# Mixture of experts: two half buckets of 768 rows per group become one bucket of 1408 rows with four overflow tiles

## The chip, the cores and the metric

The kernel runs on one core of a Trainium2 chip. The metric is device time in microseconds (us) of one execution; lower is better. Three runs of the kernel before took 3005.65, 3010.7 and 3010.94 us, so its median is 3010.7 us. A profile was taken from a separate execution.

## The reference, cut to what matters

2048 tokens (16 batches of 128 rows, 512 wide) pass through five stages: a state space scan, a cross attention, a ternary feed-forward, a self attention with a gated cross attention, and a mixture of experts, each with a residual and a layernorm. The change is in the last stage:

```python
scores = softmax(x @ gate_w.T); topk_w, topk_idx = top_k(scores, 8)   # 64 experts
w_e = zeros(N, 64).at[arange(N)[:, None], topk_idx].add(topk_w)
flat = w_e[:, inv_map]                      # N x 8 groups x 8 experts
scalar = flat.sum(-1)                       # N x 8: zero where no expert of the group was chosen
soft = softmax(where(flat == 0, -1e9, flat))
xg = x[:, None] + einsum('ngi,ghi->ngh', soft, mask_up_w)
a = silu(einsum('ngh,gih->ngi', xg, gate_proj_w)) * einsum('ngh,gih->ngi', xg, up_proj_w)
y = einsum('ng,ngh->nh', scalar, einsum('ngi,ghi->ngh', a, down_proj_w))
x = layernorm(x + y)
```

A token needs only the groups in which it has an expert, on average two thirds of the eight. Each group has its own weights (gate and up 512 x 352, down 352 x 512, mask_up 8 x 512).

## The kernel before, in words

The 16 batches live in SBUF as `k.x[b]`. `Moe.route` (L1688) takes two batches at a time: it finds the experts, a row's position in each group (`pos`, with the running count `off`), and builds `row`, 776 numbers per token (x, the soft weights split in two for TensorE, and the eight shares). `scatter` (L1792) then writes each batch with one indirect DMA per group from GpSimd (L1797) into `bucket[half][group]`, which holds 768 rows; rows that are not in the group have a destination out of bounds and are dropped. The first eight batches are routed during the attention stage, the other eight in the first units of the expert stage.

`stage_moe` (L1997) works through **units** of two tiles of 128 bucket rows (`pair`): for each half, eight groups of three units (768 rows are 6 tiles). The last group of the second half scatters only batches 8 to 11 (`LAST = 3` tiles: a unit of two and one of one), and works on the `HELD = 4` batches 12 to 15 whole and in place (`placed`, two units). That is 49 units and 97 tiles. One unit is:

- `fetch` (L1821): the rows come in by a DMA from SP, three units ahead;
- `places` and `turn_in` (L1839, L1847): `pts` turns the soft weights, `px` adds the mask product to the turned rows, ScalarE and VectorE copy it to `xgT`;
- `rest` (`pr`, L1874), `gate` (`pg`, L1889; then `pta`, L1899) and `up` (`pu`, L1889): the three matrix products; ScalarE takes silu, VectorE multiplies into `act` (L1905);
- `down` and `store` (`y`, L1913; `yo`, L1926): the product down, scaled by the share, written to `results` by a DMA from ScalarE's queue (L1927).

TensorE's order is pinned: pr(t), pg(t), pta(t), pu(t), pts(t+2), px(t+1), y(t). Half a unit after a tile is stored, `combine` (L1941) has GpSimd gather its results for a batch (`got`, L1935, an indirect DMA; a row that is not in the group reads row 0, which is zero) and add them to `k.x[b]` (L1948). Tile j serves batch j of its half; the last tile of a bucket serves all that remain, so three gathers and adds come at once. After the last group, `combine_last` (L1957) gathers, adds and calls `ended` (L1967), which does a batch's layernorm in pinned VectorE order by `GROUPS` (L1965) and sends it out. The batches of the first half are normalised earlier, by `finish`.

Weights of a group are loaded one group ahead; a mask matrix is prepared by `prepare` (L1660). If a bucket overflows, a flag read on the chip takes a branch at the end (`tc.If(over > 0)`) that does all groups for all batches in place. `clear_rows` (L605) zeroes the buckets in the second stage.

Of the kernel before, what the change touches and what calls it, by code (L numbers as in the profile page):

```python
# [10 lines left out]
F32 = mybir.dt.float32  # L11
# [593 lines left out]
def clear_rows(k, pool):  # L605
# [9 lines left out]
    for h in range(2):  # L615
        for bucket, result in zip(k.bucket[h], k.results[h]):
            k.nc.sync.dma_start(result[0:1], k.zeros[0:1, 0:D])
            for j in range(Moe.TILES):
                k.nc.sync.dma_start(bucket[j * P : (j + 1) * P], k.zeros)
                yield  # L620
# [975 lines left out]
class Moe:  # L1596
# [6 lines left out]
    CAP = 768  # L1603
    TILES = CAP // P
    LAST, HELD = 3, 4

    def __init__(self, k, pp):
# [3 lines left out]
        self.off = [None, None]  # L1611
# [76 lines left out]
    def route(self, p):  # L1688
# [72 lines left out]
        for i in range(2):  # L1761
            off = wr.tile([P, NG], F32, tag=f"r_off{half}", name="r_off", bufs=2)
            if self.off[half] is None:
                nc.vector.tensor_copy(pos[:, i], pc[:, 0, i])
                nc.vector.tensor_copy(off, pc[:, 1, i])
            else:
                nc.vector.tensor_tensor(pos[:, i], pc[:, 0, i], self.off[half], ALU.add)
                nc.vector.tensor_tensor(off, pc[:, 1, i], self.off[half], ALU.add)
            self.off[half] = off
        if p == (NB - self.HELD) // 2 - 1:  # L1770
            self.last = wr.tile([P, 1], F32, name="r_last")
            nc.vector.tensor_scalar(self.last, off[:, NG - 1 :], float(self.CAP - P * self.LAST), None, ALU.add)
        to = wr.tile([P, 2, NG], I32, tag="r_to", name="r_to", bufs=2)
        t = wr.tile([P, 2, NG], F32, tag="r_tt", name="r_tt", bufs=2)
        nc.vector.tensor_scalar(t, ind, -4096.0, 4096.0, ALU.mult, ALU.add)
        nc.vector.tensor_tensor(to, t, pos, ALU.add)
        nc.vector.scalar_tensor_tensor(t, pos, float(self.CAP), ind, ALU.is_lt, ALU.mult)
        nc.vector.scalar_tensor_tensor(self.gidx[:, 2 * p : 2 * p + 2], pos, 1.0, t, ALU.add, ALU.mult)
        if half and p < (NB - self.HELD) // 2:
            at = self.gidx[:, 2 * p : 2 * p + 2, NG - 1 :]  # L1780
            nc.vector.tensor_scalar(at, at, float(P * self.LAST), None, ALU.min)

# [6 lines left out]
        self.sending.append(self.scatter(p, rows, to))  # L1789
        yield  # L1790

    def scatter(self, p, rows, to):  # L1792
        k, nc, half = self.k, self.nc, p // (NB // 4)
        for i, row in enumerate(rows):
            nc.sync.dma_start(k.rows[2 * p + i], row)
            for g in range(self.NG - (p >= (NB - self.HELD) // 2)):
                nc.gpsimd.indirect_dma_start(  # L1797
                    out=k.bucket[half][g][:, :], out_offset=bass.IndirectOffsetOnAxis(ap=to[:, i, g : g + 1], axis=0),
                    in_=row[:, :], in_offset=None, bounds_check=self.CAP - 1, oob_is_err=False,
                )  # L1800
                if g % 2:
                    yield


    def pair(self, h, g, j, n, to=True):
# [434 lines left out]
```

## Time and profile before

| what | value |
| --- | --- |
| median of three runs | 3010.7 us (3005.65 to 3010.94) |
| the profiled execution | 2989.28 us |
| its span, first to last instruction | 2987.5 us |
| TensorE's granted clock over the span | 0.993 |
| last stage: first unit's pr to the end | 2144.6 to 2987.5 us |

The span is what the profile's columns add up in; the profiled execution is 0.7% below the median. TensorE (PE) is busy for most of it. VectorE is DVE, ScalarE is ACT, GpSimd is POOL, SyncE's DMA queue is SP. A matmul of 32-bit floats appears as two instructions in the trace. The chain of waits names, at each moment, the work that the end was waiting for.

### The profile page before, as it was taken

The numbers are of one execution on the slowest core, as the hardware profiler recorded it, in microseconds if no ns is written. First come the engines' busy times: TensorE is split into PE (matmuls) and PEld (weight loads), VectorE is DVE, ScalarE is ACT, GpSimd is POOL, SyncE is SP. The second block draws the span as 40 slices with busy tenths as digits, with TensorE's granted clock in tenths as the row PEclk, the third lists the DMA queues.
The fourth block names the chain that finished last, engine by engine and source line by source line (L and its number), as shares of the span: only waits on it lengthen the run. The fifth ranks groups of instructions, "written<-read, shape, count | busy, mean of one in ns | idle before, by whom it ended". The sixth has DMA issues, their size and how long they took to land.

```text
span 2987.5 us, 41364 instructions
## 1 busy us (share of the span) xinstructions
PE 2892.0 (97%) x14354; PEld 1941.5 (65%) x14378; DVE 1882.1 (63%) x4181; ACT 1322.1 (44%) x3239; POOL 1478.3 (49%) x1264
## 2 busy tenths in 40 slices
PE   8999999999999999999999989999999999999998
PEld 6666665555555555555787556666677777777776
DVE  6999997776676676656887797666652322141213
ACT  6887884333343343345444797555522211111111
POOL 7999996433334334332333664246536653333332
PEclk9999999999999999999999999999999999999999
DMA  7655454870000000014000200224257765464542
GB/s 207 210 136 129 132 134 135 281 261 15 8 11 11 8 11 11 8 54 159 1 1 1 72 1 1 61 102 163 110 201 251 255 220 177 158 206 157 179 152 86
DMA packets 172319, 334.16 MB, mean 112 GB/s; under 512 B 22053, under 2 KB 80933, under 8 KB 170566
## 3 DMA queue, kind: packets, MB, share of 16 engines
q1 hardware_dynamic: 126630, 219.51, 24.0%
q0 software_dynamic: 19840, 66.30, 6.2%
q10 hardware_dynamic: 25632, 45.62, 4.1%
q8 instruction: 116, 1.90, 0.3%
q14 instruction: 101, 0.83, 0.1%
HBM read 245.22 MB, written 139.81 MB: 129 GB/s over the span
## 4 chain that ended last, share of the span: by engine, by line
PE 75%; DVE 14%; ACT 3%; issue 2%; POOL 1%; DMA 1%; SPq 0%; DVEq 0%; ACTq 0%; POOLq 0%
PE y L1913 8%; PE pq L706 7%; PE po L826 6%; PE pu L1889 5%; PE pg L1889 5%; PE pkv L66 4%; PE pr L1874 4%; PE po L1038 4%; PE ao L815 3%; PE sc L775 3%; PE py L66 2%; PE pt L566 2%; PE po L66 2%; PE pg L1018 2%; PE pu L1018 2%
## 5 line engine op out<-in xcount | busy, mean ns | idle before, releaser
L795 POOL TENSOR_TENSOR pr<-pr,sm 128x512 f32<-128x512 f32 x128 | 135.6, 1059 | 367.6 <-DVE sm L794 280.1
L1935 POOL DMA_INDIRECT got<-results,gidx x124 | 119.6, 965 | 392.1 <-DMA results<-yo 366.0
L66 POOL TENSOR_TENSOR dBx<-dtx,BC 128x1024 f32<-128x1024 f32 (+1 forms) x131 | 300.7, 2317 | 17.6 <-DMA BC<-bcd 9.3
L788 ACT ACTIVATE pr<-sc,mx,sf 128x256 f32<-128x256 f32 x256 | 142.4, 561 | 332.7 <-DVE mx L781 304.0
L66 ACT ACTIVATE h<-dt,negA 128x254 f32<-128x254 f32 x512 | 244.1, 477 | 16.7
L826 PE MATMUL po<-w,aT 128*128 128x512 f32 x512 | 233.1, 593 | 0.8 <-DVE aT L820 0.8
L706 PE MATMUL pq<-w,xT 128*128 128x512 f32 x512 | 230.5, 593 | 0.6 <-DVE m L672 0.6
L1913 PE MATMUL y<-dn,act 128*128 128x512 f32 x388 | 182.6, 593 | 3.8 <-DVE act L1905 3.8
L1905 DVE TENSOR_TENSOR act<-pu,act 128x512 f32<-128x512 f32 (+1 forms) x49 | 33.6, 685 | 240.5 <-PE pu L1889 220.7
L66 DVE TENSOR_TENSOR_SCAN h<-h,dBx 128x1024 f32<-128x1024 f32 x72 | 164.9, 2291 | 27.2 <-ACT h L66 22.0
L677 POOL TENSOR_TENSOR m<-m,m 128x512 f32<-128x512 f32 x96 | 122.7, 1278 | 111.9 <-DVE m L672 108.5
L1889 PE MATMUL pu<-xgT,gu 128*128 128x256 f32 (+1 forms) x784 | 177.8, 380 | 0.0
L1889 PE MATMUL pg<-xgT,gu 128*128 128x256 f32 (+1 forms) x784 | 175.5, 377 | 0.0
L1948 POOL TENSOR_TENSOR x<-got,x 128x512 f32<-128x512 f32 x120 | 151.4, 1278 | 46.5 <-DMA got<-results,gidx 45.5
L1926 DVE TENSOR_SCALAR yo<-y,row 128x512 f32<-128x512 f32 x93 | 69.8, 751 | 163.8 <-PE y L1913 160.2
L66 PE MATMUL pkv<-w,cT 128*128 128x512 f32 x368 | 167.3, 597 | 1.3 <-DMA w<-in_x_wvT 1.3
L1028 POOL TENSOR_TENSOR lo<-sg,hi 128x512 fp32r<-128x512 f32 x64 | 84.3, 1319 | 153.4 <-ACT hi L1027 153.3
L826 PEld LDWEIGHTS po<-w,aT 128*128 128x128 f32 x512 | 94.6, 190 | 100.7 <-issue 96.6
L706 PEld LDWEIGHTS pq<-w,xT 128*128 128x128 f32 x512 | 94.0, 190 | 101.3 <-issue 92.3
L1889 PEld LDWEIGHTS pg<-xgT,gu 128*128 128x128 f32 x784 | 146.5, 190 | 17.4
L1889 PEld LDWEIGHTS pu<-xgT,gu 128*128 128x128 f32 x784 | 145.2, 192 | 18.0
L1797 POOL DMA_INDIRECT bucket<-r_row,r_to x124 | 123.0, 992 | 52.7 <-issue 34.9
(408 smaller groups left out, 6886.9 us busy)
## 6 DMA issues: line engine op xcount, KB each, us to landing
bucket<-zeros SPq DMA_DIRECT2D x96, 388.0 KB, 8.0
row<-bucket SPq DMA_DIRECT2D x46, 776.0 KB, 5.7
BC<-bcd SPq DMA_DIRECT2D x128, 256.0 KB, 5.3
results<-yo ACTq DMA_DIRECT2D x93, 256.0 KB, 2.9
gu<-in_moe_guT SPq DMA_DIRECT2D x16, 1408.0 KB, 6.2
x_k<-kv ACTq DMA_DIRECT2D x32, 256.0 KB, 4.7
x_v<-kv ACTq DMA_DIRECT2D x32, 256.0 KB, 5.1
v<-x_v SPq DMA_DIRECT2D x32, 256.0 KB, 2.9
```

Of the source, the lines that this page charges most:

```text
L66: return self.tc.keep_in_program_order(call(*args, **kw))
L677: nc.gpsimd.tensor_tensor(m1, m1, m2, ALU.add)
L706: nc.tensor.matmul(ps, src[:, c], w[c], start=c == 0, stop=c == KC - 1)
L788: nc.scalar.activation(pr[:, j], st.sc[g, i][:, j], AF.Exp, scale=st.sf[:, h : h + 1], bias=st.mx[g, i][:, j : j + 1], accum_out=sm[:, j : ...
L795: nc.gpsimd.tensor_tensor(pr, pr, sm.unsqueeze(2).to_broadcast([P, 2, 2 * P]), ALU.mult)
L826: nc.tensor.matmul(st.po, aT[:, j], k.wo[h // 8][:, h % 8], start=h == 0, stop=h == G * J - 1)
L1018: nc.tensor.matmul(p[:, e], w[:, c, at : at + P], sn.qT[:, :, c], start=c == 0, stop=c == KC - 1)
L1797: nc.gpsimd.indirect_dma_start(out=k.bucket[half][g][:, :], out_offset=bass.IndirectOffsetOnAxis(ap=to[:, i, g : g + 1], axis=0), in_=row[ ...
L1889: self.nc.tensor.matmul(ps[:, e, 0:n], gu[:, c, at : at + P], u.xT[:, c, 0:n], start=c == 0, stop=c == KC - 1)
L1913: self.k.tc.keep_in_program_order(self.nc.tensor.matmul(y, aT, dn[:, c], start=c == 2, stop=c == 1))
L1935: nc.gpsimd.indirect_dma_start(out=got[:, :], out_offset=None, in_=self.k.results[h][g][0:end, :], in_offset=bass.IndirectOffsetOnAxis(ap= ...
L1948: self.nc.gpsimd.tensor_tensor(k.x[b], got, k.x[b], ALU.add)
```

## The change

Both halves now share one bucket of `CAP = 1408` rows (11 tiles) per group, kept as two DRAM tables, for tiles 0 to 4 and 5 to 10. The first pass does tiles 0 to 4 of each group (units of 2, 2 and 1), from the rows of batches 0 to 7; the second pass does tiles 5 to 10 (three units of 2). Rows of batches 5 to 7 whose place is beyond row 640 are scattered a second time into the later table (`remainder`), from the start of the stage.

A row of batch 11 or later whose place is beyond 1408 goes into a table `over`, one tile of 128 rows per group, by a further scatter per batch and group (`EDGE = 11`, groups 0 to 6). `slots` finds on the chip which groups went beyond 1408, up to four, and after each of the groups 3 to 6 of the second pass comes one unit of one tile (`beyond`): its rows and its weights are gathered by indirect DMAs from GpSimd (`pick`, `load_over`) with indices from `slots`, and its results are gathered for batches 11 to 15 (`combine_over`). All four units run whether a group went beyond or not; the branch at the end is taken when they do not suffice. The weights use the buffers of the very first group.

The last group scatters batches 0 to 13 (`LAST = 10`) and does two batches in place (`HELD = 2`), 14 and 15. Batches 0 to 3 are normalised when the first pass ends, 4 to 15 with the last group in new `GROUPS`; batches 9 to 13 are called on in `store`, right after batch 14's result (`found`). Routing of the later eight batches begins one unit earlier.

Tiles per pass: 8 x 5 = 40; then 7 x 6 = 42, 5 of the last group, 4 overflow tiles and 2 in place. That is 93 tiles in 53 units: 40 units of two tiles and 13 of one.

```diff
-    for h in range(2):
-        for bucket, result in zip(k.bucket[h], k.results[h]):
-            k.nc.sync.dma_start(result[0:1], k.zeros[0:1, 0:D])
-            for j in range(Moe.TILES):
-                k.nc.sync.dma_start(bucket[j * P : (j + 1) * P], k.zeros)
-                yield
+    for result in k.results + k.over_results:
+        k.nc.sync.dma_start(result[0:1], k.zeros[0:1, 0:D])
+    for bucket in [b for both in k.bucket for b in both] + [k.over]:
+        for j in range(bucket.shape[0] // P):
+            k.nc.sync.dma_start(bucket[j * P : (j + 1) * P], k.zeros)
+            yield
...
-    CAP = 768
-    TILES = CAP // P
-    LAST, HELD = 3, 4
+    FIRST, TILES, OVER = 5, 11, 4
+    CAP = TILES * P
+    LAST, HELD = 10, 2
+    EDGE = TILES
...
+        if p == NB // 4 - 1:
+            nc.vector.tensor_scalar(off, off, float(self.FIRST * P), None, ALU.max)
...
+        if not half and 2 * p + 1 >= self.FIRST:
+            later = wr.tile([P, 2, NG], I32, tag="r_la", name="r_la", bufs=2)
+            nc.vector.tensor_scalar(pos, t, float(self.FIRST * P), 8192.0, ALU.is_lt, ALU.mult)
+            nc.vector.tensor_tensor(t, t, pos, ALU.add)
+            nc.vector.tensor_scalar(later, t, float(-self.FIRST * P), None, ALU.add)
+            self.later += [(rows[i], later, i) for i in range(2) if 2 * p + i >= self.FIRST]
+        over = None
+        if 2 * p + 1 >= self.EDGE:
+            far = self.far[:, 2 * p - self.EDGE + 1 : 2 * p - self.EDGE + 3]
+            nc.vector.tensor_scalar(far, pos, float(1 - self.CAP), 0.0, ALU.add, ALU.max)
+            nc.vector.tensor_tensor(far, far, ind, ALU.mult)
+            over = self.fixed.tile([P, 2, NG], I32, tag="r_ov", name="r_ov", bufs=2)
+            nc.vector.tensor_scalar(pos, t, float(self.CAP), 8192.0, ALU.is_lt, ALU.mult)
+            nc.vector.tensor_tensor(t, t, pos, ALU.add)
+            nc.vector.tensor_tensor(over, t, self.const[:, 2].unsqueeze(1).to_broadcast([P, 2, NG]), ALU.add)
...
+    def scatter(self, p, rows, to, over):
+        k, nc = self.k, self.nc
         for i, row in enumerate(rows):
-            nc.sync.dma_start(k.rows[2 * p + i], row)
-            for g in range(self.NG - (p >= (NB - self.HELD) // 2)):
-                nc.gpsimd.indirect_dma_start(
-                    out=k.bucket[half][g][:, :], out_offset=bass.IndirectOffsetOnAxis(ap=to[:, i, g : g + 1], axis=0),
-                    in_=row[:, :], in_offset=None, bounds_check=self.CAP - 1, oob_is_err=False,
-                )
+            b = 2 * p + i
+            nc.sync.dma_start(k.rows[b], row)
+            for g in range(self.NG - (b >= NB - self.HELD)):
+                self.put(k.bucket[g][b // (NB // 2)], row, to, i, g)
+                if b >= self.EDGE and g < self.NG - 1:
+                    self.put(k.over, row, over, i, g)
...
+    def remainder(self, row, to, i):
+        for g in range(self.NG):
+            self.put(self.k.bucket[g][1], row, to, i, g)
+            if g % 2:
+                yield
...
+    def slots(self):
+
+        nc, pool, NG, S = self.nc, self.fixed, self.NG, self.OVER
+        off = self.off
+        ex = pool.tile([P, NG], F32, name="ov_ex")
+        nc.vector.tensor_scalar(ex, off, float(self.CAP), None, ALU.is_gt)
+        nc.vector.memset(ex[:, NG - 1 :], 0.0)
+        rank = ex
+        for step in (1, 2, 4):
+            more = pool.tile([P, NG], F32, name=f"ov_rank{step}")
+            nc.vector.tensor_copy(more, rank)
+            nc.vector.tensor_tensor(more[:, step:], rank[:, step:], rank[:, : NG - step], ALU.add)
+            rank = more
...
+        for s in range(S):
+            nc.vector.scalar_tensor_tensor(self.one[:, s], rank, float(s + 1), ex, ALU.is_equal, ALU.mult)
+            nc.vector.tensor_scalar(least[:, s], rank, float(s), None, ALU.is_le)
...
+        for s in range(S):
+            own = pool.tile([P, n, NG], F32, tag="ov_own", name="ov_own")
+            nc.vector.tensor_tensor(own, self.far, self.one[:, s].unsqueeze(1).to_broadcast([P, n, NG]), ALU.mult)
+            row = pool.tile([P, n], F32, tag="ov_row", name="ov_row")
+            nc.vector.tensor_reduce(row, own, AX.X, ALU.add)
+            nc.vector.tensor_scalar(self.back[:, s], row, float(P), None, ALU.min)
...
+    def pick(self, out, table, s, i, rows=P):
+
+        self.nc.gpsimd.indirect_dma_start(
+            out=out, out_offset=None, in_=table, in_offset=bass.IndirectOffsetOnAxis(ap=self.at[0:rows, s, i : i + 1], axis=0)
+        )
+
+    def load_over(self, s):
+
+        nc, a, I, wr = self.nc, self.k.args, self.I, self.wr
+        gu = wr.tile([P, KC, 2 * I], F32, tag="gu", name="gu")
+        dn = wr.tile([P, 3, D], F32, tag="dn", name="dn")
+        raw = self.wk.tile([P, D], F32, tag="got", name="mup_raw", bufs=8)
+        self.over_w[s] = gu, dn
+        flat = lambda t: t.rearrange("g r c -> (g r) c")
+        for c in range(KC):
+            self.pick(gu[:, c], flat(a["moe_guT"]), s, c)
+        self.pick(raw[:, :], flat(a["moe_mup"]), s, 7)
+        yield
+        mup = self.over_mup[s] = wr.tile([P, D], F32R, tag="raw", name="mup_over")
+        for c in range(3):
+            rows = P if c < 2 else I - 2 * P
+            self.pick(dn[0:rows, c], flat(a["moe_downT"]), s, KC + c, rows)
+        nc.sync.dma_start(dn[I - 2 * P :, 2], self.k.zeros[0 : 3 * P - I, 0:D])
+        yield
+        nc.scalar.copy(mup, raw)
+        nc.vector.tensor_tensor(raw, raw, mup, ALU.subtract)
+        yield
+        nc.vector.tensor_scalar(raw, raw, self.part[:, 1:2], None, ALU.mult)
+        nc.vector.scalar_tensor_tensor(mup, mup, self.part[:, 0:1], raw, ALU.mult, ALU.add)
...
+    def beyond(self, s):
+
+        u = Ctx()
+        u.s, u.n, u.to = s, 1, [self.k.over_results[s][1:, :]]
+        return u
+
     def fetch(self, u):
         u.row = self.wk.tile([P, 2, self.ROW], F32, tag="row", name="row", bufs=self.depth)
+        if u.s is not None:
+            self.pick(u.row[:, 0], self.k.over[:, :], u.s, 7)
+            return
...
+            own = self.wk.tile([P, self.NG + 1], F32, tag="own", name="own", bufs=1)
+            self.nc.vector.tensor_tensor(own[:, 1:], u.row[:, 0, D + 4 * self.E :], self.one[:, u.s], ALU.mult)
+            self.nc.vector.tensor_reduce(own[:, 0:1], own[:, 1:], AX.X, ALU.add)
+            shares = [own[:, 0:1]]
...
-                self.ended(u.b + i)
+                for b in (*self.found, u.b + i):
+                    self.ended(b)
+                self.found = []
...
+    def combine(self, g, b):
+
+        got = self.result(g, b)
+        for _ in range(3):
+            yield
+        self.add(b, got)
+        if g == self.NG - 1 and b < self.FIRST - 1 and b % 2:
+            for _ in range(6):
                 yield
-            self.finish(b - 1, k.tc.keep_in_program_order)
-
-    def combine_last(self, ns):
-
-        k = self.k
-        found = [self.gather(1, self.NG - 1, n) for n in ns]
-        for b, got in found:
-            self.nc.gpsimd.tensor_tensor(k.x[b], got, k.x[b], ALU.add)
-        for b, _ in found:
-            self.ended(b)
-
-    GROUPS = (8, 9), (10, 11, 12), (13, 14, 15)
+            self.finish(b - 1, self.k.tc.keep_in_program_order)
+
+    def combine_over(self, s, b):
+        got = self.gather(self.k.over_results[s][:, :], self.back[:, s, b - self.EDGE + 1 : b - self.EDGE + 2])
+        for _ in range(3):
+            yield
+        self.add(b, got)
+
+    def combine_last(self, bs):
+
+        for b, got in [(b, self.result(self.NG - 1, b)) for b in bs]:
+            self.add(b, got)
+
+    GROUPS = (4, 5, 6), (7, 8), (9, 10), (11, 12, 13), (14, 15)
...
+        for q in range(2 * NG):
+            h, g = divmod(q, NG)
+            first[len(units)] = q
+            lo, hi = (m.FIRST, m.LAST if g == NG - 1 else m.TILES) if h else (0, m.FIRST)
+            for j, n in cuts(lo, hi):
+                units.append(m.pair(g, j, n))
+                units[-1].q = q
+            s = q - 2 * NG + 1 + m.OVER
+            if 0 <= s < m.OVER:
+                units.append(m.beyond(s))
+        m.sending += [m.remainder(*job) for job in m.later]
         units += [m.placed(NG - 1, b, 2) for b in range(NB - m.HELD, NB, 2)]
-        units[0] = m.opened
-        per = T // 2
+        units[-1].q = 2 * NG - 1
...
+            if u.s is not None:
+                for b in range(m.EDGE, NB):
+                    running.append(m.combine_over(u.s, b))
+                return
             j = u.j + i
-            if u.h and u.g == NG - 1:
-                m.combine_last(range(j, j + 1 if j < m.LAST - 1 else H - m.HELD))
-            else:
-                for n in range(j, j + 1 if j < T - 1 else H):
-                    running.append(m.combine(u.h, u.g, n))
+            if u.g == NG - 1 and j >= m.FIRST:
+                bs = list(range(j, j + 1 if j < m.LAST - 1 else NB - m.HELD))
+                m.combine_last(bs)
+                m.found += bs
+                if j < m.LAST - 1:
+                    for b in m.found:
+                        m.ended(b)
+                    m.found = []
+                return
+            for b in range(j, j + 1 if j < T - 1 else NB):
+                running.append(m.combine(u.g, b))
+            if u.g == NG - 1 and j == m.FIRST - 1:
+                m.found += [j]
...
+            if t + 3 == start[NG]:
+                assert not (m.now or m.sending or k.to_route)
+                running.append(m.slots())
+            if t == start[NG] + 5:
+                over = nc.values_load(m.flag, min_val=0, max_val=1)
+                running.append(m.load_over(0))
+            if unit(t - 1) and units[t - 1].s is not None and units[t - 1].s + 1 < m.OVER:
+                running.append(m.load_over(units[t - 1].s + 1))
...
+                u.w = weights[u.q] if u.s is None else m.over_w[u.s]
...
-    k.bucket = [[dram.tile([Moe.CAP, Moe.ROW], F32, name=f"bucket{h}{g}") for g in range(Moe.NG)] for h in range(2)]
-    k.results = [[dram.tile([Moe.CAP + 1, D], F32, name=f"results{h}{g}") for g in range(Moe.NG)] for h in range(2)]
+    cut = Moe.FIRST * P
+    k.bucket = [[dram.tile([n, Moe.ROW], F32, name=f"bucket{g}{i}") for i, n in enumerate((cut, Moe.CAP - cut))] for g in range(Moe.NG)]
+    k.over = dram.tile([Moe.NG * P, Moe.ROW], F32, name="over")
+    k.results = [dram.tile([Moe.CAP + 1, D], F32, name=f"results{g}") for g in range(Moe.NG)]
+    k.over_results = [dram.tile([P + 1, D], F32, name=f"over_results{s}") for s in range(Moe.OVER)]
```

## The prediction

> **What bounds the kernel now.** I read the page first: TensorE is busy for 97% of the span, and three quarters of the chain of waits is TensorE.
>
> ```profile
> PE 2892.0 (97%) x14354; PEld 1941.5 (65%) x14378; DVE 1882.1 (63%) x4181; ACT 1322.1 (44%) x3239; POOL 1478.3 (49%) x1264
> PE 75%; DVE 14%; ACT 3%; issue 2%; POOL 1%; DMA 1%; SPq 0%; DVEq 0%; ACTq 0%; POOLq 0%
> ```
>
> A share of the span says little about one stage, so next came the busy time by window in the expert stage. The columns are PE, PEld, DVE, ACT, POOL, clock, DMA share, GB/s.
>
> ```profile
> 2460.00:2600.00 140.00, 140.00 (x654) 108.72 (x653) 26.79 (x42) 18.69 (x44) 51.74 (x47) 1.00 0.52 176
> 2660.00:2940.00 280.00, 279.29 (x1302) 214.69 (x1301) 63.35 (x117) 36.72 (x87) 102.76 (x93) 1.00 0.49 165
> ```
>
> TensorE idles 0.71 us in 420; VectorE and GpSimd are idle for three quarters and two thirds. The stage is as long as its matmuls, so a tile costs what its matmuls cost. The chain near the end holds both kinds of unit, two tiles (from 2919.49) and one tile (from 2935.45):
>
> ```profile
> 2919.49 2.60 PE pr L1874 x16
> 2922.09 3.45 PE pg L1889 x16
> 2925.54 0.22 PE pta L1899 x2
> 2925.76 3.46 PE pu L1889 x16
> 2929.22 0.22 PE pts L1843 x2
> 2929.44 0.40 PE px L1854 x4
> 2929.83 0.46 PE px L1860 x4
> 2930.29 5.15 PE y L1913 x12
> 2935.45 1.30 PE pr L1874 x8
> 2936.75 1.78 PE pg L1889 x16
> 2938.53 0.11 PE pta L1899
> 2938.64 1.79 PE pu L1889 x16
> 2940.43 0.22 PE pts L1843 x2
> 2940.64 0.47 PE px L1854 x4
> 2941.12 0.87 PE px L1860 x8
> 2941.99 2.58 PE y L1913 x6
> ```
>
> pts and px work for later units, so the third pair of rows is that of the one-tile unit (0.40 + 0.46) and the last that of two tiles (0.47 + 0.87). Two tiles: 2.60 + 3.45 + 0.22 + 3.46 + 0.22 + 0.47 + 0.87 + 5.15 = 16.44 us; the y rows of the quiet second half lie 16.45 apart, and I use that. One tile: 1.30 + 1.78 + 0.11 + 1.79 + 0.11 + 0.40 + 0.46 + 2.58 = 8.53, that is 0.30 over half of two.
>
> **The change, part by part.** *Tiles.* Before: 48 x 16.45 + 8.53. After: 40 x 16.45 + 13 x 8.53. Difference 8 x 16.45 - 12 x 8.53 = 131.6 - 102.4 = 29.2 us less. An overflow unit turns soft weights twice: 4 x 0.11 = 0.4 back. **-28.8.**
>
> The pg row speaks for the one-tile unit: 16 instructions in 1.78 us against 3.45, 111 ns each against 216. [...]
>
> *The end.* Before, only two batches are normalised after the last unit's first y. After, batch 14's product releases, in pinned VectorE order, the norms of 9 to 13, 14 and 15. The last unit's pr begins at 2960.80; batch 14's sum follows 12.60 us later (2973.40). From the end of the chain: a sum takes 0.78 with its gap, statistics 0.95 a batch (2976.76 to 2977.71), a group's inverse root 2.36 (2977.71 to 2980.07). So 12.60 + 0.78 + 7 x 0.95 + 3 x 2.36 + 0.78 = 27.9 against 19.25 (2980.05) before: +8.6. One ScalarE pass fewer follows (0.72): **+7.9.** GpSimd doesn't set this: the gather came 3.1 us after the one-tile unit's y (2947.68 - 2944.57); five at 1.27 and five adds at 1.24 end at 3.1 + 6.3 + 6.2 = 15.6, before batch 13's turn near 19.6.
>
> *Norms of 4 to 8.* They fall in the last group's units. The root of (4, 5, 6) stands on VectorE ahead of `rest` of the one-tile unit: 0.75 + 0.95 + 2.36 + 0.36 = 4.4 us after its start, where pta is due at 1.30 + 1.78 = 3.1: 1.4 us. Adds still queued on GpSimd can hold it longer, up to 11 x 1.24 = 13.6. I take **+3** (0 to +15), nearer the queue's empty end, because GpSimd idles two thirds now.
>
> *Collisions.* One row shows VectorE held by GpSimd:
>
> ```profile
> 2221.01 5.37 DVE L1749 TENSOR_TENSOR r_ex<-r_ex,r_on 128x128 f32<-128x128 f32 x1
> 2221.27 4.95 POOL L1948 TENSOR_TENSOR x<-got,x 128x512 f32<-128x512 f32 x4
> ```
>
> The same instruction takes 0.28 to 0.29 otherwise; here it ends with GpSimd's four adds, `act` is late, and TensorE idles 3.1 us. The first pass now ends a group with one gather, not three: **-3.1** (0 if another burst takes its place). In the second pass the bursts grow to six adds (7.4 us) and five, and VectorE gets two-input work there: two in `load_over` and `own`, 12 in all. At 3.1 each that is 37 us, with the 6.5 us that VectorE idles ahead of `act` in a two-tile unit it is nothing. I take **+3**, a quarter of a hit per overflow unit's three, nearer the idle row.
>
> *Small things.* `route` gets some 3 to 10 tiny VectorE instructions per pair (0.17 to 0.44 us each) and `slots` about 40; they lie in VectorE's idle time ahead of `act`, which is only 3 us in a one-tile unit: **+1.5** (0 to +8, one microsecond for each such unit of the first pass). The 24 second scatters open the stage on GpSimd: **+1.5** (0 to +25, see the rivals). Twelve result rows are zeroed at once, 5 us of SP's queue at 516 us; TensorE waits there for no load: 0 (to +5). Data volume hardly grows: the software queue's 66.30 MB less 124 gathers of 0.26 MB is 33.8 MB, about 10900 rows of 3.1 KB, the rows that the routing picks; so out-of-range rows move nothing.
>
> *GpSimd's own load.* First pass: 24 + 62 + 35 scatters at 1.28 (0.98 and 0.30 of issue) and 40 gathers with adds at 2.51 make 255 us; the pass is 16 x 16.45 + 8 x 8.53 + some 18 of routing = 350. Covered. Second pass, group with overflow unit: 16 gathers and adds 40.2, nine picks at 1.28 (a scatter's row) 11.5, together 51.7 of 3 x 16.45 + 8.53 = 57.9. Covered, by little; GpSimd is busy 37% of this time now. The first pick is queued three units ahead of its use, the weights four.
>
> *Sum.* -28.8 + 7.9 + 3 - 3.1 + 3 + 1.5 + 1.5 = **-15.0 us** on the profiled 2989.3. I carry the difference to the median: 3010.7 - 15.0 = **2995.7**.
>
> **Rivals.** *Full cover:* VectorE and GpSimd hide everything but the tail: 3010.7 - 28.8 - 3.1 + 7.9 = 2986.7. For it: VectorE is busy only 20 to 23% of the second pass (the windows above). Against: the `r_ex` row.
>
> *Stalls eat it:* hits on every overflow unit (12 more), the norms held by bursts (6 more): -15 + 18 gives 3014; half of it 3005. For it: two-input work meets larger bursts. Against: most of it lands where VectorE idles.
>
> *GpSimd becomes the bound (slower):* place, the second pass from group 3; the price is a pick of 128 rows of 2816 bytes. From (57.9 - 40.2) / 9 = 1.97 us a pick, GpSimd no longer ends its work in the period, the overflow rows and weights come late and TensorE waits. At 3 us it falls behind by 4 x 9 x 1.03 = 37: 3010.7 - 15 + 37 = 3033. For it: 90% of GpSimd's time is spoken for, in order, with waits for results between. Against: a scatter of 3104 bytes a row takes 0.99, a gather of 2048 bytes 0.97, so the row's length hardly counts.
>
> *The opening:* the 24 scatters come ahead of GpSimd's last attention add (2158.07) and its two clears, for which the first rows and `rest` wait: 24 x 1.28 = 31 less the 6.2 us that it idles there: 3010.7 - 15 + 25 = 3021. From 17 scatters ahead the gain is gone. Against: the adds stand first in the program.
>
> *The change doesn't do what it says:* the four tiles don't suffice and the branch redoes everything: 64 units x 16.45 = 1053 more, 4049. Counted from the reference's inputs (drawn with seed 0), three groups exceed 1408 rows (1461, 1415, 1469, below 1536), and the last group has 1236 of 1280 rows before its held batches: very unlikely.
>
> **How the numbers follow.** Forecast 0.62 (2989 to 3003); full cover 0.08; stalls 0.14 (2999 to 3014); GpSimd 0.10; opening 0.05; branch 0.01. Faster by over 0.2% (below 3004.7; about what a measurement of this kernel can tell) is 0.62 + 0.08 + 0.05 of the stalls = 0.75; same is the other 0.09; slower 0.16. The range leaves out the slower cases and the lowest ends: 2982 to 3011.
>
> **What would show it.** Right: y rows of one-tile units 8.5 us apart, 93 tiles; the stage's TensorE time down by 29; no `r_ex` above 1.5 us; after the last y, a chain of VectorE norms near 12.7 us (27.9 - 15.2) instead of 4.1. Wrong: TensorE waiting for `row`, `gu` or `pts` at an overflow unit (GpSimd late); picks far above 1 us; y waiting for `act` in the second pass; a longer gap at the stage's start; or pg of one tile far above 1.78, which would undo the tile price.

## The result, and the profile after

The changed kernel took **3052.7 us** (median of four executions, 3044.5 to 3054.5), the kernel before 3009.0 beside it: ratio 1.0141, 95% interval 1.0119 to 1.0163. It is 43.8 us slower, where 15 us faster was predicted. The profiled execution took 3051.1 us. First the lines of its page that answer to those of before:

```profile
PE 2892.9 (95%) x14422; PEld 1942.0 (64%) x14446; DVE 1896.3 (62%) x4280; ACT 1327.2 (44%) x3267; POOL 1618.2 (53%) x1405
PE 60%; DVE 13%; DMA 3%; ACT 3%; issue 3%; POOL 3%; another core or an unknown queue 1%; SPq 0%; DVEq 0%; POOLq 0%; ACTq 0%
```

TensorE's share of the chain of waits fell from 75% to 60%; what came in is DMA, GpSimd, and two names that stand for "nothing the profile shows": "issue" and "an unknown queue". To place the loss I divided each profile at five events: GpSimd's first and last add of the gated attention, the first unit's last y, the last y of the first pass, the last y of all. Of the rows below only the first three belong here; the others are experiments. Times in us.

| profile | to first add | gated attention | to first y | first pass | second pass | end | span |
| --- | --- | --- | --- | --- | --- | --- | --- |
| before | 1892.0 | 267.3 | 17.0 | 396.9 | 402.7 | 11.6 | 2987.5 |
| before_again | 1897.7 | 270.8 | 17.1 | 407.7 | 402.9 | 11.6 | 3007.9 |
| **after** | 1896.8 | 288.7 | 18.1 | 351.1 | 475.3 | 19.3 | 3049.3 |
| late_remainder | 1898.2 | 270.6 | 19.6 | 367.1 | 475.8 | 19.4 | 3050.7 |
| mup_late | 1896.1 | 282.5 | 17.8 | 349.8 | 465.5 | 19.2 | 3030.9 |
| both | 1898.5 | 269.6 | 23.9 | 352.6 | 465.7 | 19.4 | 3029.6 |
| no_remainder | 1896.5 | 270.0 | 18.1 | 342.5 | 477.0 | 19.4 | 3023.5 |
| sp_weights | 1900.9 | 285.5 | 18.0 | 351.3 | 475.0 | 19.3 | 3050.0 |
| fill_puts | 1896.3 | 291.7 | 18.1 | 334.0 | 475.9 | 19.2 | 3035.3 |
| fill_all | 1896.6 | 290.6 | 16.4 | 339.5 | 476.0 | 20.8 | 3039.9 |
| first_spread | 1896.8 | 267.7 | 18.1 | 338.8 | 474.2 | 19.4 | 3014.9 |
| second_spread | 1901.7 | 280.1 | 17.0 | 338.1 | 438.7 | 18.9 | 2994.5 |
| both_spread | 1895.6 | 269.8 | 16.6 | 335.1 | 438.6 | 18.8 | 2974.7 |

Against before_again, a second profile of the kernel before at its usual time: gated attention +17.9, first pass -56.6 (the prediction's terms give about -65), second pass +72.4 (the tiles alone: +34.6), end +7.7.

*Gated attention.* GpSimd's timeline; the number in brackets is idle time ahead of the instruction:

```profile
2148.53 0.97 POOL L1824 DMA_INDIRECT bucket<-r_row,r_la  x1 [0.30 <-issue]
2149.80 0.97 POOL L1824 DMA_INDIRECT bucket<-r_row,r_la  x1 [0.30 <-DVE gate L1515]
2151.08 0.98 POOL L1824 DMA_INDIRECT bucket<-r_row,r_la  x1 [0.30 <-issue]
2152.07 1.07 POOL L1490 TENSOR_TENSOR at_s<-at_s,sm 128x512 f32<-128x512 f32 x1
...
2156.87 0.97 POOL L1824 DMA_INDIRECT bucket<-r_row,r_la  x1 [0.31 <-issue]
2157.86 1.29 POOL L1516 TENSOR_TENSOR x<-x,gate 128x512 f32<-128x512 f32 x1
```

The second scatters (`r_la`), which the program calls for at the start of the expert stage, stand between the attention's `at_s` and `x`: GpSimd works on `at_s` and `x` with no idle time ahead of them, so they were due earlier. The `gate` that the last line's `x` reads is done at 2149.65; the add starts 8.2 us later, behind five scatters and two `at_s`.

*Second pass.* After each of the first three overflow units a unit takes 24.4, 24.1 and 25.9 us instead of 16.4, and one of 23.2 stands ahead of the first. The timeline of the first of them:

```profile
2765.44 0.94 POOL L2069 DMA_INDIRECT got<-results,gidx  x1 [1.75 <-DMA results<-yo]
...
2777.93 0.95 POOL L1886 DMA_INDIRECT mup_raw<-in_moe_mup,ov_at  x1 [0.30 <-issue]
...
2781.67 0.62 ACT L1908 CAST mup_over<-mup_raw 128x512 fp32r<-128x512 f32 x1 [11.33 <-DMA mup_raw<-in_moe_mup,ov_at]
2782.20 0.59 ACT L2023 ACTIVATE act<-pg 128x512 f32<-128x512 f32 x1
...
2782.68 0.36 ACT L2028 COPY aT<-pta 128x256 f32<-128x256 f32 x1
...
2783.10 0.79 PE L1981 MATMUL px<-soft,mup 128*128 128x256 f32 x2 [5.54 <-ACT aT L2028]
```

Read it from below: TensorE waits 5.54 us for `aT`; `aT` stands on ScalarE behind `mup_over`; that copy has waited 11.33 us for the pick of `mup_raw`; and the pick was issued at 2777.93 as the last of a row of GpSimd's, six gathers from 2765.44 on and four picks of `gu`. The copy's wait began at 2770.34, 7.6 us before the pick was issued, and the first matmul that reads `mup_over` starts at 2817.97, 36 us after the copy. Over the second pass, by the list of waits (us in all, times, longest):

```profile
PE px L1981 <- ACT aT L2028: 17.5, 3, 6.1
ACT mup_over L1908 <- DMA mup_raw<-in_moe_mup,ov_at: 41.5, 4, 11.9
```

### The profile page after: what moved, and what is told of

It reads as the page before. It is cut to its first block, busy times and chain, and to the rows that moved or that the text cites. A ratio compares the mean times of both kernels' runs of the same rounds, so it can differ in the third digit from the quotient of the medians.

```text
span 3049.3 us, 41951 instructions
## 1 busy us (share of the span) xinstructions
PE 2892.9 (95%) x14422; PEld 1942.0 (64%) x14446; DVE 1896.3 (62%) x4280; ACT 1327.2 (44%) x3267; POOL 1618.2 (53%) x1405
## 4 chain that ended last, share of the span: by engine, by line
PE 60%; DVE 13%; DMA 3%; ACT 3%; issue 3%; POOL 3%; another core or an unknown queue 1%; SPq 0%; DVEq 0%; POOLq 0%; ACTq 0%
PE y L2048 7%; PE pq L706 7%; PE po L826 6%; PE pu L2016 4%; PE po L1038 4%; PE pg L2016 4%; PE pr L2001 3%; PE ao L815 3%; PE sc L775 3%; PE pt L566 2%; PE pg L1018 2%; PE pu L1018 2%; PE pT L803 1%; PE ps L1427 1%; PE pk L706 1%
## 5 line engine op out<-in xcount | busy, mean ns | idle before, releaser
L2080 POOL TENSOR_TENSOR x<-got,x 128x512 f32<-128x512 f32 x146 | 183.5, 1273 | 66.4 <-DMA got<-results,gidx 64.1
L2048 PE MATMUL y<-dn,act 128*128 128x512 f32 x372 | 179.6, 606 | 12.3 <-DVE act L2032 12.3
```

Of the source, the lines that this page charges most:

```text
L2048: self.k.tc.keep_in_program_order(self.nc.tensor.matmul(y, aT, dn[:, c], start=c == 2, stop=c == 1))
L2080: self.nc.gpsimd.tensor_tensor(self.k.x[b], got, self.k.x[b], ALU.add)
```

## The experiments

They were made in five sets; in each, before ran beside them on the same chip. In the first three sets (three chips) before took 3005.6 to 3009.9 us, in the last two (two other chips) 2988.0 and 2990.3. So a time is told with its ratio to before of its own set. The record doesn't name the chip of after and of the first profile of before.

**Set 1 (before 3009.9 us).** Four kernels. The first is before, unchanged.

> The kernel before, unchanged, profiled once more. In the trace of the changed kernel, TensorE's semaphore events come up to 7.5 us after the end of the matmul that sets them, 111 of them over 0.5 us late, all after 1986 us; in the trace of before none is. The profiled execution of before is also 20 us under its median (2989.3 against 3009.0), that of after is not (3051.1 against 3052.7). Theory A (the late wake-ups are something that executions of both kernels have, and the one profiled execution of before happened to lack): this profile has some, its span lies near 3005, and 15 to 20 us of the 62 between the two profiles are no effect of the change. Theory B (the change brings them): again none, and a span near 2988.

3009.7 us, span 3007.9, 49 late wake-ups by the count that gives 111 in after: theory A. (Some 30 records of TensorE's steps are missing in this profile and some 50 in after, so part of either count is steps without a record.) The profile that the prediction was made from lacked some 20 us that the timed executions have. The table shows where: 3.5 us in the gated attention, 10.8 in the first pass, nothing in the second. Another 5.7 lie ahead of the first add; there the profiles of the last two sets, which have no late wake-ups, differ as much (1892.7 to 1901.7), so hold-ups account for some 14 of the 20.

`late_remainder`:

```diff
-        m.sending += [m.remainder(*job) for job in m.later]
+        m.sending.append(m.remainders())     # each put inside issue_after(the clearing of rest)
```

> The changed kernel with one edit: the 24 second scatters are held behind the clearing of the expert stage's spare tiles, so that none stands in GpSimd's order ahead of the attention stage's last adds. Theory A (they stood in the way of those adds): the last add of the attention stage comes at about 2163 us and not at 2184, nearly all of that reaches the end, and the time is 3030 to 3036 against 3052.7; GpSimd then has 31 us of scatters at the start of the expert stage, which may give back up to 5. Theory B (the stage is longer because of late wake-ups, whatever GpSimd's order): the add comes at 2175 or later and the time falls by less than 8.

3047.5 us, ratio 1.0109 (1.0082 to 1.0137). The attention stage is mended as theory A says (270.6), but the time is not: the first pass is 16.0 longer. In the new place the 24 scatters run for 31 us in one piece (from 2169.5), and this is what TensorE and ScalarE do near its end:

```profile
2192.14 0.27 PE L1703 MATMUL pl<-gw,r_x 128*128 128x64 f32 x1 [1.88 <-issue]
...
2194.24 0.26 PE L1703 MATMUL pl<-gw,r_x 128*128 128x64 f32 x1 [1.83 <-issue]
...
2194.96 0.58 ACT L1994 COPY xgT<-px 128x512 f32<-128x512 f32 x1 [10.25 <-remote]
```

TensorE waits for nothing that the profile shows and yet issues one matmul in 2 us; ScalarE idles 10.25 us for a release ("remote") that no instruction's end accounts for. This made theory C, below.

`mup_late`:

```diff
+        self.pick(raw[:, :], flat(a["moe_mup"]), s, 7)      # now ahead of the four picks of gu
...
+        yield
+        yield
+        keep(nc.scalar.copy(mup, raw))
```

> The changed kernel with one edit: of the picks of an overflow tile's weights the one for mup goes first, and ScalarE's and VectorE's work on it stands later in their order, just over a unit ahead of the tile's own turn. Theory A (the second pass loses 31 us because ScalarE's copy of mup waits for a pick that stands behind six gathers and four picks on GpSimd, and ScalarE's later work waits behind the copy): the losses of 6.8, 8.0, 7.6 and 9.5 us at the four places go, 24 to 31 us in all, and the time is 3022 to 3030. Theory B (it is GpSimd's load itself, with its gathers, picks and adds in bursts, and the wait would only show at another place): less than 8 us are won.

3028.5 us, ratio 1.0054 (1.0037 to 1.0071): 24 us under after, inside theory A's range, but not for its reason. Only the first of the four places is whole in its profile, and the second pass is 9.8 us shorter; of the 18.4 us between the two spans 6.2 lie in the gated attention, which the edit doesn't touch. The units after the three overflow units take 24.6, 25.6 and 21.0 us, little less than in after, now with this:

```profile
2835.15 0.60 ACT L2024 ACTIVATE act<-pg 128x512 f32<-128x512 f32 x1 [10.28 <-remote]
```

`both` joins the two edits:

> The two edits together. If both theories A hold, the gains add: 42 to 52 us, 3001 to 3011, the time of the kernel before, give or take 0.3%. If one alone holds, 3022 to 3036. If the late wake-ups decide, over 3036.

3031.0 us, ratio 1.0066 (1.0049 to 1.0083). The gains don't add; the same waits without a visible releaser are there (VectorE's `act`: 47.4 us in four pieces for "remote", 12.3 in three in after), and the first unit's last y ends 23.9 us after the attention's last add, in after 18.1.

**Set 2 (before 3005.6).** Theory C measured by itself, in the kernel before:

```diff
+                self.nc.gpsimd.indirect_dma_start(     # table: 8 spare ones in turn; every index is 8192
+                    out=table[:, :], out_offset=bass.IndirectOffsetOnAxis(ap=self.outside[:, 0:1], axis=0),
+                    in_=self.k.ident[:, :], in_offset=None, bounds_check=P - 1, oob_is_err=False,
+                )
...
+            if t == 36:
+                m.nowhere(24)                  # burst
+            if 30 <= t < 42:
+                m.nowhere(1)                   # spread, in both halves of a unit
```

> The kernel before with one addition in a quiet place: in the second pass (unit 36 of 49) GpSimd issues 24 indirect scatters in one run, of 128 rows each, all of whose places lie outside the table, so that no row moves; nothing waits for them and the output is unchanged. Theory C (a long unbroken run of GpSimd's indirect transfers itself holds up the wake-ups and the issue of the other engines, whatever it moves): TensorE, ScalarE and VectorE stand for some 8 to 17 us inside the 31 us of the run, with waits that no instruction ends, and the time rises by 8 to 17 us over before (3009.9), to 3018 to 3027. Theory D (the stalls come of the bytes on the DMA rings, of the buffers or of GpSimd's in-order queue): gathers and adds come up to 31 us late, which 9 buffers cover, and the time rises by less than 3.

> The same 24 empty scatters in the kernel before, one in each half of units 30 to 41, between the gathers and adds that stand there. Theory C: there is no long run, and the time stays within 3 us of before (3007 to 3013). A theory C' (each indirect transfer costs the others its 0.5 us, however it is spaced) expects the same rise as the run in one piece, 8 to 17. Theory D: within 3 us.

`burst` took 3030.4 us, ratio 1.0082 (1.0065 to 1.0099): **24.8 us for 24 transfers that move nothing.** `spread` took 3006.1, ratio 1.0003 (0.9994 to 1.0013). Theory C, with more than its 8 to 17 us, and not C'. (That rows out of range move nothing is the prediction's estimate: before's scatters moved some 10900 rows of the 124 x 128 = 15872 that they name. Here every place is out of range.) TensorE's, ScalarE's and SP's timelines of burst, whose run goes from 2795.90 to 2826.61:

```profile
2809.39 2.76 PE L1874 MATMUL pr<-gu,xgT 128*128 128x192 f32 x16
2811.06 7.44 ACTq L1927 DMA_DIRECT2D results<-yo  x2
2834.16 0.33 ACT L1878 ACTIVATE rest<-pr 128x192 f32<-128x192 f32 x1 [28.92 <-remote]
```

```profile
2794.59 23.89 SPq L1825 DMA_DIRECT2D row<-bucket  x2
```

A line with x2 goes from the start of the first issue to the end of the second. One issue of `results` by itself takes 0.33 us (at 2793.92), in before one of `row` 0.38 (median; 1.18 at most), so what is late is the second. `rest` starts 22.0 us after the end of the products that it reads (2812.15), and 7.6 us after the run's end. The unit takes 37.4 us instead of 16.4.

> The changed kernel without the 24 second scatters; left out are the rows of blocks 5 to 7 whose place in a group is 640 or more, so the output is not the full one. With the scatters held behind the attention stage (the run late_remainder) the attention stage was 18.1 us shorter and the first units 16.0 longer. Theory C: the same 24 transfers cost 16 to 18 us in either place, and without them the time is 3052.7 - 17 = 3033 to 3037. Rival: what was lost in the first pass there had another cause (a late gather, a late weight), and the time here is that of late_remainder, 3042 to 3050.

3022.5 us, ratio 1.0056 (1.0039 to 1.0073): 30 us less than after, or 26.8 by the two distances to before (43.8 and 17.0). In the profiles 18.7 of it is in the gated attention and 8.6 in the first pass. That is more than the 16 to 18 us that theory C expected; the 8.6 us in the first pass are put down to the run, which is argued.

`sp_weights` loads the overflow weights by SyncE:

```diff
-            self.pick(gu[:, c], flat(a["moe_guT"]), s, c)
+        nc.sync.dma_start(gu, a["moe_guT"][s].rearrange("(c p) i -> p c i", p=P))
+        nc.sync.dma_start(raw, a["moe_mup"][s])
```

> The changed kernel with the weights of the four overflow tiles loaded by SyncE from groups 0 to 3 and not picked by GpSimd from the groups found (32 picks less, four rows' picks remain); the bytes are the same, only rows of overflow tiles are computed with other weights than they should be. Theory C (eight picks more in one run with six gathers make it long enough to hold up the other engines; taking mup's copy out of the way removed the wait for the pick at the first tile only): the losses of 6.8, 8.0, 7.6 and 9.5 us at the four places go, 26 to 32 us, and the time is 3021 to 3027. Theory D (the bytes of the weights beside those of the gathers): the losses stay, less than 8 us are won.

3043.0 us, ratio 1.0121 (1.0105 to 1.0138); the second pass stays at 475.0, as theory D's number has it. But ScalarE's copy, left in its place, still waits 31.1 us in three pieces (the profile puts one down to `mup_raw`, two to `over_results<-yo`). At the first overflow unit SyncE issues `mup_raw` at 2758.40 and the copy starts at 2769.25. So who issues the transfer changes little as long as the copy stands close behind (31.1 us of waits for 41.5 in after); against bytes as the reason speaks `second_spread` below, on another chip, which makes as many transfers as after and whose second pass takes 438.7 us, 1.4 over before's 402.7 and the tiles' 34.6.

**Set 3 (before 3006.5).** Pauses instead of moves: a clearing of 512 bytes on one partition (0.51 us) behind each indirect transfer.

```diff
+        with tc.issue_after(dma.ins):
+            self.pause = nc.gpsimd.memset(self.pad, 0).ins      # the next transfer is queued behind it
```

> The run burst (24 empty scatters in one piece in the kernel before, which cost 24.8 us against before), with a short clearing of 512 bytes on one partition by GpSimd behind each of them, some 0.3 to 0.6 us by the clearing of 256 words in 0.28 us at the stage's start. Theory C as a rate (indirect transfers asked for at 1.28 us each, without a pause, are more than what serves them can take, the excess piles up and others wait; a little slower they are taken): the rise falls to 0 to 6 us, 3006 to 3012. Theory C as a count (24 without other long work between is too many, at this pace or a little slower): 15 to 25 us remain, 3020 or more.

3007.7 us, ratio 1.0005 (0.9992 to 1.0018), and no unit beside the run takes over 16.5 us in its profile. With half a microsecond of other work behind each of the 24 there is next to nothing left of the 24.8 us of set 2: a rate, not a count, if burst would have cost as much on this chip. It wasn't run here; for it speaks that before takes 3006.5, as in set 2.

> The changed kernel with the same short clearing behind each scatter, scatters kept in the order of the program, and the 24 second ones row by row, so that they come to stand partly between the first units' gathers. Theory C (rate): the attention stage and the first pass lose what they lose to runs of scatters, 18 us and some 10 us, as in the run without the second scatters (3022.5): 3010 to 3024. Rival (GpSimd's own time is what counts there: 88 clearings in the attention stage and the opening lengthen its work by some 40 us, and its adds end that stage): 3035 or more.

3038.8 us, ratio 1.0118 (1.0097 to 1.0139): in the rival's range. The first pass is the shortest of all (334.0), as theory C has it, but the gated attention is longer (291.7 us; 288.7 in after). The rival puts this down to GpSimd's own time: its 88 clearings, at the 0.51 us that one takes, are an estimated 45 us more in the attention stage and the opening.

> The run mup_late (3028.5) with the clearing behind every indirect transfer, scatter, gather and pick. Theory C (rate): the second pass also keeps some 25 us, and the time is 2985 to 3002, under the kernel before. Rival (the second pass's losses behind the overflow tiles are of the bytes or of ScalarE's order): no more than the scatters' share, 3004 to 3012. Rival (GpSimd's longer queue): 3012 or more.

3043.6 us, ratio 1.0134 (1.0113 to 1.0155): worse than mup_late's 1.0054. GpSimd is busy 356 of the second pass's 476 us (264 of 475 in after), and VectorE's `own` waits 39.0 us in four pieces for the rows of the overflow tiles. The last rival, GpSimd's longer queue, is right here.

> The kernel before with the clearing behind each scatter and gather. Its one quiet profile is 20 us under its usual time, and its usual profile (the run before_again) has 58 late wake-ups, all beside runs of scatters. Theory C (rate): 2985 to 2997. Rival (these late wake-ups are chance, or the longer queue costs what the pauses give): 3000 to 3012.

2996.1 us, ratio **0.9970 (0.9958 to 0.9981)**: the pauses alone make the kernel before faster by 10.5 us. In its profile the first pass takes 395.5 us (407.7 in before_again), the gated attention 277.2 (270.8).

**Set 4 (before 2990.3).** Spreading without pauses where GpSimd is loaded. In `second_spread`:

```diff
+        picks((raw[:, :], flat(a["moe_mup"]), s, 7))       # then a yield
+        picks(*gus[:2])                                    # and so on: five halves of units
...
+                    running.append(m.combine_over(u.s, b, (b - m.EDGE) // 2))
+                running.append(m.combine(u.g, b, (b - j) // 2))
```

> The changed kernel with the 24 second scatters behind the attention stage, row by row between the first units' gathers, and with the clearing behind each of them and behind each scatter of the expert stage; the scatters of the attention stage are as they were. Theory C (runs hold the others up; the attention stage lost 18 us to the 24 that stood in it, the first pass some 17 to its runs): the attention stage takes 270 us, the first pass 334 to 340, and the time is 3052.7 - 18 - 14 = 3018 to 3024. Rival (the 24 cost their 16 us wherever they stand, as in late_remainder, paced or not): 3034 or more.

> The changed kernel with the second pass's transfers of an overflow tile spread: its eight picks go out over five halves of units and not two, mup's copy stands a unit later, and the gathers of the last tile of a group and of an overflow tile go out in twos, a half apart, behind the adds before them. The number of transfers is the same. Theory C (the 23 to 25 us that stay at the four places are runs of up to 20 transfers): the second pass goes from 475 to 445 us or less, and the time is 3018 to 3028. Rival (GpSimd has too much to do there at any order: 25 transfers of 1.28 us and 16 adds of 1.27 us in the 58 us of such a group, 52 us): the losses stay or move, and the time is over 3030, no better than mup_late's 3028.

> Both edits together. If theory C is the cause in both stretches, the gains add, 3052.7 - 32 - 28 = 2985 to 2998, under the kernel before (3006.5). If one alone holds, 3016 to 3028.

> The run burst with 12 empty scatters in one piece and not 24. In burst the last wake-up that came in time was at 2810 us, 16 us and 12 transfers into the run. If a run costs only what comes after that point, 12 cost 0 to 4 us. If each transfer of a run costs the same, 12 cost half of 24.8 us, 10 to 14.

`first_spread` 3017.4 us, ratio 1.0098 (1.0074 to 1.0121); `second_spread` 2989.2, 0.9995 (0.9981 to 1.0010); `both_spread` **2978.1, ratio 0.9962 (0.9949 to 0.9975)**, 12.2 us under before and the fastest of all; `burst12` 2991.2, 1.0005 (0.9995 to 1.0016). In these four profiles there are 0 to 1 late wake-ups, and burst12 is no test of length, since before has none either. But the second pass of first_spread is as long as ever (474.2), and its waits in the second pass name the copy:

```profile
PE px L1996 <- ACT aT L2043: 17.0, 3, 6.2
```

```profile
ACT mup_over L1923 <- DMA mup_raw<-in_moe_mup,ov_at: 34.4, 3, 12.0
```

(the numbers: us in all, times, longest). In second_spread TensorE's longest wait there is another:

```profile
PE y L2058 <- DVE act L2042: 1.1, 1, 1.1
```

So on this chip the second pass's loss is the order of two queues and not the hold-up by runs. Which of the edits does it, the later copy, the spread picks or the spread gathers, isn't separated: mup_late ran on a chip with hold-ups only.

**Set 5 (before 2988.0).**

> The run burst once more (24 empty scatters in one piece in the kernel before), beside burst12. If the kernel before takes about 3006 us here: 3026 to 3036, as at first. If it takes about 2990: theory C as a property of any chip expects 10 to 25 us over it; theory E (the hold-up shows on some chips or in some placements only, those on which the kernel before takes 3006) expects less than 3.

> The run burst12 once more (12 in one piece), beside burst. If the kernel before takes about 3006 us here: 0 to 4 us over it if only what comes after some 12 transfers of a run counts, 10 to 14 if each transfer of a run costs the same. If it takes about 2990: less than 3, as at first.

`burst_same` 2991.1 us, ratio 1.0012 (1.0000 to 1.0024), `burst12_same` 2989.3, 1.0000 (0.9990 to 1.0010). That is nearer theory E: the run that cost 24.8 us on one chip costs 3.2 by the medians on another, just over the 3 that E allowed and far from C's 10. In the profile of burst_same no unit beside the run takes over 16.5 us.

## Why the prediction was wrong, point by point

- **Tiles, -28.8: right.** In after a one-tile unit takes 9.1 us behind a two-tile unit of 16.0, 25.1 together, and 16.45 + 8.53 = 24.98 was said. In both_spread, where little else is left, the passes are 61.8 shorter and 35.9 longer than in the quiet profile of before.
- **The end, +7.9: right.** 11.6 became 19.3, +7.7.
- **Norms of 4 to 8, +3: low.** The last group's second and third unit take 21.9 and 10.2 us for 16.4 and 8.5: +7, held by GpSimd's adds (a norm's statistics wait up to 9.4 us for one), inside the range given. In both_spread it is +1.
- **Collision gone, -3.1: right.** `r_ex` takes 1.15 us at most. (VectorE's share in the two windows of the prediction is 19 and 23%, not 20 to 23.)
- **The second scatters "open the stage on GpSimd": +1.5: wrong.** The rival had the mechanism and nearly the price (25; 26.8 without the scatters, of which it didn't foresee the part in the first pass), and was given 0.05, "against: the adds stand first in the program". The failing step is this sentence: the order on GpSimd was not that of the program. Moving them out of the attention stage shortens that stage by 10.3 us without hold-ups (280.1 to 269.8), by 18.1 with them (288.7 to 270.6).
- **"Covered, by little ... The first pick is queued three units ahead of its use, the weights four": wrong, and the largest error.** The picks are as cheap as said (0.95 us against a bound of 1.97), GpSimd has the time (busy 264 of the second pass's 475 us), and in that pass TensorE's two waits are for `aT` and `act`, none for `row` or `gu`. (In the code the weights of the later three tiles are queued three units ahead, not four.) But the use that counted wasn't the tile's matmul; it was the first instruction that reads the pick, ScalarE's copy, which came due 7.6 us before its pick was issued. `aT`, behind it on ScalarE, started at 2782.68, 9.0 us after the end of the product that it reads (`pta`, 2773.65). The second pass is 38 us over the tiles' price (475.3 - 402.7 - 34.6), and on one chip 35.6 of the pass's time go when copy, picks and gathers are spread (474.2 in first_spread, 438.6 in both_spread).
- **New collisions, +3: wrong in kind.** The wait asked for, y for `act`, is there (10.3 us in the second pass), but not beside an add on GpSimd: 4.8 us come once, at the first place, where `act` stands on VectorE behind its half of the work on `mup_over`, and 5.0 in the last group, where `act` stands behind a norm's statistics that wait 9.4 us for an add of GpSimd; these belong to the norms.
- **The difference carried to the median: wrong.** The profile lacked what the runs had, some 14 us of hold-ups among 20, and the change adds to just these.

How far do the two orders explain the 43.8 us? On the chip of set 4, whose profiles show 0 to 1 late wake-ups, mending them is worth 39.3 us (3017.4 - 2978.1) and 11.1 (2989.2 - 2978.1). The changed kernel itself wasn't run there; if the two add, it would take 3028.5, 38 over before. With both mended it is 12.2 under, near the 15.0 that the sum gave without them, though with pauses and spread gathers that the sum didn't have. On the chip of set 1 (49 late wake-ups in before_again) mending both orders (`both`) still leaves 21 us over before (3031.0 beside 3009.9). That these are hold-ups by runs of transfers is argued from the waits without a releaser; no run there mends both orders and also deals the transfers out.

## What to carry to other kernels

For every transfer that a change adds, look for the first instruction on each engine that reads what it brings, and place that one, not only the transfer: here a copy of 0.6 us, whose result no matmul read for 36 us, cost some 8 us a time (units of 24.4, 24.1 and 25.9 us for 16.4), as `aT` stood behind it on ScalarE. Read the order on the engine, not in the program: here the second scatters stood ahead of another stage's last adds, one of which started 8.2 us after its `gate`. Where GpSimd issues many indirect transfers, deal them out: on the chip of set 2, 24 cost 24.8 us in one piece and 0.5 when spread, though on that of set 5 the piece cost 3.2. Pauses between them made the kernel before 10.5 us faster (set 3), but not the changed one where GpSimd was busy 356 of 476 us (fill_all, 37 us over before). Take a second profile before trusting one that is 0.7% under the median.

## What the runs showed of the hardware

On one chip (set 2), 24 indirect transfers in one piece, one every 1.28 us, cost 24.8 us: ScalarE's `rest` came 22 us after the products that it reads. In late_remainder, on another (set 1), two matmuls beside such a run started 2.1 us apart. On a third (set 3) 0.51 us of other work behind each left 1.2 us. On the chip of set 5 the unpaused run cost 3.2 us, and on that of set 4, where only 12 were tried, 0.9. Bytes aren't the cause in burst, as by the estimate beside it none moved. In the profiles from the three chips, and in after, the records of semaphore steps of VectorE, ScalarE and GpSimd are 75 to 199 fewer than the instructions that make a step (of these VectorE's in after: 3789 records for 3909 instructions), and TensorE's are fewer too (in after 1853 for 1905); in those from the other two, and in the first profile of before, they are never fewer. So records are missing in the profiles in which engines start late; that the one has to do with the other is not shown. Whether an execution without recording is held up too, and what makes chips differ, no run here shows.
